# Preparing blocks 1 to 3 of the first attention earlier, loading expert weights in larger steps, and splitting a bias later

## The chip, the cores and the metric

The kernel runs on one core of a Trainium2 chip. A core has five engines that run side by side and wait for each other by semaphores: TensorE (PE in the profile; its weight loads are PEld), VectorE (DVE), ScalarE (ACT), GpSimd (POOL) and SyncE (SP), which here only starts transfers. Each engine works through its own list of instructions in order. The metric is the device time of one execution in microseconds (us). The kernel before took 1230.82 us, the median of six runs (1230.57 to 1233.02).

## The reference

The input x has four sequences of 512 tokens with 256 features. Four layers follow each other, each reading a layernorm of x and added to x:

```python
x = L0_attn_x                                    # (4, 512, 256)
x = x + L0_attn(layernorm(x), w_project, w_out)  # 16 heads of 16, causal, 512 keys
x = x + L0_ffn(layernorm(x), router_w, router_b, expert_w, expert_b)
x = x + L1_attn(layernorm(x), w_qkv, w_proj)     # over the leading axis, heads of 128
x = x + L1_ffn(layernorm(x), gate, up, down)     # weights packed in four bits
```

The second layer is a mixture of eight experts with a router for every feature: 2048 logits a token, softmax over the eight experts of each feature, the two greatest kept and made to sum to one, and the eight expert outputs added with these weights:

```python
logits = (h @ router_w.T + router_b).reshape(T, O, E)
w, sel = top_k(softmax(logits, -1), 2);  w = w / w.sum(-1, keepdims=True)
c = zeros((T, E)).at[t, sel].add(w)              # summed over the features
out = einsum("te,teo->to", c, einsum("th,eoh->teo", h, expert_w) + expert_b)
```

## The kernel before

The 2048 tokens stand in SBUF as 16 tiles of 128 rows (`xres`); four tiles make a block of 512 rows, and block j holds tokens 128j to 128j+127 of all four sequences. The first attention goes over the blocks in 44 steps, called batches in the code: 4 for block 0, 8 for block 1 and 16 each for blocks 2 and 3. All products are in float32.

Before its first step a block is prepared (`prepare`): its rows are normalised (`norm_pieces`: statistics on DVE, an inverse root by Newton steps, `rsqrt_steps`, on DVE for blocks 0 and 1 and on POOL for blocks 2 and 3, then the normalised rows `xn`), transposed on PE and evacuated as `xT0`, projected (`project`: queries and keys, two halves of two products, evacuated by ACT to `stage` and laid out in `qk` by eight transfers a half, L558) and given values (`values`, L570). The zeros and ones that stand between the heads in `qk` and `va` come from POOL (`blank`, five parts a block).

A step n then does, on PE, `greatest(n+1)` (scores whose maxima DVE takes, L633 and L653), `shift(n)` (the maxima transposed, L664, and subtracted from the queries by DVE, L669), `mask(n+1)` (the causal mask added by products, L648), some filling work, `mixed(n-1)` (probabilities times values, L719), `powers(n)` (scores again, transposed, L683), and filling work again. ACT makes the exponentials (L692) and POOL sets their masked part to zero (L702). The score tiles come from five PSUM buffers; a `greatest` and a `powers` take four each. After the last batch of a sequence `divided` transposes, divides and transposes again (L737 to L755, one buffer `oq`), and after the last sequence multiplies by `w_out` (L764) and adds to `xres`.

The order on PE, DVE and POOL is written out by hand. Filling work is a list of streams of pieces. A piece names an engine and a cost; `fill(PE=..., DVE=...)` advances a slot counter and issues pieces, earlier streams first, until the budget is spent. A piece can also ask for a number of slots since the one before it and for a condition. The streams of this stage are the preparation of the next block (put first), `fold_pieces` (the biases are added to the expert and router weights: a product of a selector with the split bias `bp`, L269, and two additions on DVE, L275, for each of eight pieces), `hidden_pieces` (the layernorm and transposes for the mixture), `logit_pieces` (L251, evacuated by ACT), `weight_pieces` (17 pieces a tile on DVE: the two greatest, and the sums), `result_pieces` (expert products, L251) and `addition_pieces`. A logit piece waits for all folds of its pair, for the weights of the tile two before, and for a count of weight pieces made. All these evacuate through `ps_dn`, two PSUM buffers that also serve the transposes and projections.

The split of the biases, three bfloat16 parts in `rows`, is made on POOL at the start (`blanks`, L521 to L532) from a 96-row array that the host lays out with the rows repeated three times. The weights of router and experts are loaded in 16 transfers of 256 KB, two after each of the first eight steps (`load_pair`), the last two blocks of x after steps 2 and 6. The order on SP is not written out: a scheduler places its transfers, and each waits for the transfer that used its semaphore before.

After the last step the second attention (L890 to L1025) runs with what is left of the mixture as filling work, a share for each of its steps that is computed from the products left, and then the last layer.

## Time and profile before

| | us |
|---|---|
| median of six runs | 1230.82 |
| the profiled execution | 1231.05 |
| its span, first to last instruction | 1229.3 |
| PE busy | 1172.2 (95%) |
| DVE busy | 812.8 (66%) |
| ACT busy | 483.7 (39%) |
| POOL busy | 131.3 (11%) |
| first scores (`greatest(0)`) start | 25.9 |
| powers of step 0, 3, 7 and 10 end | 38.2, 74.8, 114.4, 142.4 |
| first product of router logits starts | 134.7 |
| powers of step 43 end | 401 |
| weights of the second attention are loaded | from 419.9 |

The profile page gives the busy time of the engines, a strip of 40 slices, the chain of work that ended last, and the costliest groups of instructions. The trace behind it can be asked for a timeline of a stretch, for waits, and for busy times by stretches. In all of them a product of float32 counts as several PE instructions, and a PE that is shown busy may run at a lower granted clock.

### The profile page before, as it was taken

What the parts mean: (1) busy time and instruction counts of PE and PEld (TensorE: products, weight loads), DVE (VectorE), ACT (ScalarE), POOL (GpSimd) and SP (SyncE); (2) the same over time, 40 slices, a digit from 0 to 9 for tenths busy, and PEclk for the clock granted to TensorE, in tenths of its full rate; (3) what the DMA queues carried; (4) which work ended last, traced back from release to release, by engine and by line L of the source; (5) the groups of instructions that cost most, each with busy time, mean ns of one, the idle gap of its engine ahead of it and who ended that gap; (6) DMA issues with size and microseconds to landing.
All of it is one profiled execution on the core that took longest, in us unless ns stands there. A gap on an engine that the chain in (4) does not pass through costs nothing.

```text
span 1229.3 us, 18921 instructions
## 1 busy us (share of the span) xinstructions
PE 1172.2 (95%) x7278; PEld 682.4 (56%) x7278; DVE 812.8 (66%) x1862; ACT 483.7 (39%) x1101; POOL 131.3 (11%) x249
## 2 busy tenths in 40 slices
PE   6888999999999897999999999999999999999998
PEld 4656555555545443555555555555645456475487
DVE  3655589888889838395967396588589962734710
ACT  1243455555545533344444344345234431312300
POOL 7343422111121001000000000100000000000000
PEclk9899999999999988999999999999999999999999
DMA  6031102000000310000000001011010000000000
GB/s 201 6 100 35 19 1 36 1 1 2 1 2 2 116 56 1 1 1 1 1 1 1 1 1 35 10 43 53 1 50 19 1 1 17 1 1 18 0 1 35
DMA packets 19386, 26.78 MB, mean 22 GB/s; under 512 B 4992, under 2 KB 13440, under 8 KB 19040
## 3 DMA queue, kind: packets, MB, share of 16 engines
q1 hardware_dynamic: 18624, 24.40, 7.1%
q10 hardware_dynamic: 672, 1.18, 0.3%
q8 instruction: 57, 0.93, 0.3%
q14 instruction: 33, 0.27, 0.1%
HBM read 19.27 MB, written 2.10 MB: 17 GB/s over the span
## 4 chain that ended last, share of the span: by engine, by line
PE 76%; DVE 17%; ACT 3%; issue 1%; POOL 1%; DMA 0%; ACTq 0%; DVEq 0%; POOLq 0%
PE qk_ps L937 10%; PE y L1178 9%; PE g L874 9%; PE u L874 9%; PE o L1025 8%; PE lg_ps L251 7%; PE eo L251 6%; DVE mx L653 4%; PE s L633 4%; PE s L683 2%; PE v_ps L919 2%; PE qk_ps L548 2%; PE av L719 2%; PE s L950 1%; DVE lg L411 1%
## 5 line engine op out<-in xcount | busy, mean ns | idle before, releaser
L937 PE MATMUL qk_ps<-xT,wqkv 128*128 128x512 f32 x320 | 151.3, 605 | 5.1 <-ACT qT L941 5.1
L251 PE MATMUL lg_ps<-rw,xT 128*128 128x512 f32 x256 | 127.2, 620 | 4.4 <-ACT part L339 1.4
L251 PE MATMUL eo<-ew,xT 128*128 128x512 f32 x256 | 121.2, 598 | 1.9 <-ACT part L339 1.9
L1025 PE MATMUL o<-wpj,oT 128*128 128x256 f32 x512 | 119.4, 382 | 0.0
L653 DVE TENSOR_REDUCE mx<-s 128x1 f32<-128x384 f32 (+3 forms) x176 | 100.5, 633 | 18.1 <-PE s L648 18.1
L1178 PE MATMUL y<-wd,it 128*128 128x256 f32 x512 | 112.1, 379 | 0.0
L1025 PEld LDWEIGHTS o<-wpj,oT 128*128 128x128 f32 x512 | 96.0, 190 | 28.2 <-issue 16.4
L1178 PEld LDWEIGHTS y<-wd,it 128*128 128x128 f32 x512 | 97.0, 190 | 15.6 <-issue 2.9
L937 PEld LDWEIGHTS qk_ps<-xT,wqkv 128*128 128x128 f32 x320 | 59.6, 191 | 75.4 <-issue 61.8
L692 ACT ACTIVATE pt<-s 128x512 f32<-128x512 f32 (+1 forms) x176 | 83.7, 561 | 35.5 <-PE s L683 35.5
L874 PE MATMUL g<-xT,wgu 128*128 128x512 f32 x192 | 90.5, 594 | 0.0
L874 PE MATMUL u<-xT,wgu 128*128 128x512 f32 x192 | 90.2, 592 | 0.0
L702 POOL TENSOR_SCALAR_AFFINE_SELECT pt<-pt 128x256 f32<-128x256 f32 (+2 forms) x88 | 56.7, 651 | 267.2 <-ACT pt L692 266.8
L339 ACT ACTIVATE part<-eo,c 128x256 f32<-128x256 f32 x128 | 53.7, 472 | 77.3 <-PE eo L251 77.3
L1156 ACT ACTIVATE th<-sq 128x512 f32<-128x512 f32 x64 | 40.3, 630 | 88.7 <-DVE sq L1155 88.7
L251 PEld LDWEIGHTS lg_ps<-rw,xT 128*128 128x128 f32 x256 | 47.0, 196 | 50.2 <-issue 39.0
L251 PEld LDWEIGHTS eo<-ew,xT 128*128 128x128 f32 x256 | 47.1, 191 | 47.8 <-issue 40.0
L633 PE MATMUL s<-qk 32*128 32x128 f32 (+3 forms) x512 | 67.5, 500 | 2.0 <-ACT pt L692 1.9
L239 DVE TENSOR_TENSOR xres<-xres,y 128x256 f32<-128x256 f32 x16 | 6.7, 421 | 91.3 <-PE y L1178 91.3
L313 ACT COPY lg<-lg_ps 128x512 f32<-128x512 f32 x64 | 37.7, 589 | 72.5 <-PE lg_ps L251 72.5
L366 DVE TENSOR_TENSOR part<-part 128x512 f32<-128x512 f32 x32 | 21.9, 684 | 64.2 <-ACT part L339 64.1
L941 ACT COPY qT<-qk_ps 128x512 f32<-128x512 f32 x64 | 37.8, 593 | 61.5 <-PE qk_ps L937 61.5
(254 smaller groups left out, 1821.7 us busy)
## 6 DMA issues: line engine op xcount, KB each, us to landing
qk<-stage SPq DMA_DIRECT2D x56, 64.0 KB, 2.4
wqkv<-in_w_qkv SPq DMA_DIRECT2D x2, 1536.0 KB, 8.2
rw<-in_router_w SPq DMA_DIRECT2D x8, 256.0 KB, 4.4
ew<-in_expert_w SPq DMA_DIRECT2D x8, 256.0 KB, 5.2
wpj<-in_w_proj SPq DMA_DIRECT2D x1, 2048.0 KB, 15.3
out<-xres SPq DMA_DIRECT2D x4, 512.0 KB, 2.6
xres<-in_x SPq DMA_DIRECT2D x3, 512.0 KB, 7.1
dq_wgu<-in_gate_w SPq DMA_DIRECT2D x8, 128.0 KB, 2.4
```

The costliest lines, as they stand in the source:

```text
L251: nc.tensor.matmul(ps, lhsT=xT[:, hc, (g % 4) * P : (g % 4 + 1) * P], rhs=w[:, hc, 2 * pair : 2 * pair + 2, :].rearrange("p e o -> p (e o) ...
L339: nc.scalar.mul(part[:, e % 4], ps[:, i], c[:, e : e + 1])
L633: nc.tensor.matmul(tiles[h][:, b * nk : (b + 1) * nk].rearrange("p (c k) -> p c k", k=P), lhsT=queries(j, g)[r, s], rhs=qk[r, g, : j + 1, ...
L653: nc.vector.tensor_reduce(maxes[n % 2][:, :nb, h, 0], ps[:, : nb * nk].rearrange("p (b k) -> p b k", b=nb), AX.X, ALU.max,)
L692: nc.scalar.activation(pt[:, i, : nb * nk], tiles[2 * pair + i][:, : nb * nk], AF.Exp, scale=0.25)
L702: nc.gpsimd.affine_select(out=last, in_=last, compare_op=ALU.is_ge, fill=0.0, base=0, pattern=pattern, channel_multiplier=-1,)
L874: nc.tensor.matmul(ps, lhsT=wgu[:, w, half, jj, par * P : (par + 1) * P], rhs=xT[:, half, :], start=half == 0, stop=half == 1,)
L937: nc.tensor.matmul(ps, lhsT=wqkv[:, hc, kv, h, :], rhs=xT[:, hc, :], start=hc == 0, stop=hc == 1,)
L941: nc.scalar.copy(kT if h == HPK else qT[:, h, :], ps)
L1025: nc.tensor.matmul(ys[t // 2][:, t % 2], lhsT=state["o"][:, h, t * P : (t + 1) * P], rhs=wpj[:, HPK * kv + h, :], start=kv == 0 and h == 0 ...
L1156: nc.scalar.activation(th, sq, AF.Tanh, scale=0.7978845608028654)
L1178: nc.tensor.matmul(ps, lhsT=it[:, c // 2, c % 2, t * P : (t + 1) * P], rhs=wd[:, c // 2, c % 2, :], start=c == 0, stop=c == 2 * NJ - 1,)
```

## The change

- Block 1 is normalised right after block 0, on DVE, before the first step; its transposes stand between `greatest(0)` and `mask(0)`, and DVE evacuates them. Its projections and values are a stream of their own that begins between `mask(0)` and `greatest(1)`. Its `xT0` takes an unused buffer of the logits.
- The preparation of block 2 is put in at step 1 and that of block 3 at step 8, where block 2 came at step 4 and block 3 at step 12. Both use POOL for the Newton steps; values come before queries and keys; conditions hold the projections back until enough steps and blanks are done.
- `blank` has six parts a block instead of five; POOL makes two after step 0 and then one a step. `blanks` waits for the rows of block 1 rather than those of block 0.
- The bias array has 8 rows; it is loaded three times into a buffer that DVE sets to zero first. Its split, in three parts, is made on POOL after steps 1, 2 and 3, and uses buffers of the mixture.
- The weights of router and experts are loaded four transfers after each of steps 0 to 3. A fold waits for four slots after its load instead of three, and for slot 11.
- Block 2 of x is loaded at the start, before the first step.
- `hidden_pieces(0)` is put first among the streams and does its Newton steps on DVE; the two output products of block 0 lose a gap between their pieces.

```diff
@@ fold_pieces
-                    "DVE", 1.4, cond=lambda i=i, c=c: slot >= loaded.get((i, c), slot) + 3
+                    "DVE", 1.4,
+                    cond=lambda i=i, c=c: slot >= max(loaded.get((i, c), slot) + 4, 11),
@@ hidden_pieces
-        yield from norm_pieces(b, b1, b2, out, cond=lambda: b < 2 or done in halves)
+        yield from norm_pieces(
+            b, b1, b2, out, eng=None if b else nc.vector, cond=lambda: b < 2 or done in halves
+        )
@@ blank
-            if i == 4:
+            if i == 5:
                 to = va.shape[1] if j == NBLK - 1 else (j + 1) * per_block
                 nc.gpsimd.memset(va[:, j * per_block : to], 1.0)
-                nc.gpsimd.memset(keys[96:97], 1.0)
@@ the bias buffer
-        bs = a3.tile([P, 2, 512], F32, tag="pt", name="bs")
-        nc.sync.dma_start(out=bs[0:96], in_=bias)
+        bs = b1.tile([P, 2, 512], F32, tag="hi4", name="bs")
+        nc.vector.memset(bs, 0.0)
@@ blanks, and the new bias_pieces
-            for i in range(5):
+            for i in range(6):
                 blank(1, i)
+        def bias_pieces():
             d = bs[0:96, 0]
...
             nc.gpsimd.tensor_copy(bp[0:32], bh[0:32])
+            yield
             nc.gpsimd.tensor_tensor(br, d, bh, ALU.subtract)
...
             nc.gpsimd.tensor_copy(bp[64:96], br[64:96])
+            yield
             for i in range(8):
                 nc.gpsimd.tensor_copy(sel[:, i, :], mask32[:, i : i + 1].to_broadcast([P, P]))
@@ prepare, cut into three
+        def inputs_T(j, xn, xT):
             for hc in range(2):
                 yield need("PE", 0.5, 1 - hc)
-                ps = transposed(out[0], hc, ps_dn, "dn", f"x0_ps{j}_{hc}")
-                nc.scalar.copy(
+                ps = transposed(xn, hc, ps_dn, "dn", f"x0_ps{j}_{hc}")
+                copy = nc.vector.tensor_copy if j == 1 else nc.scalar.copy
+                copy(
...
+        def projections(j, xT):
+            if j > 1:
+                for s in (0, 2):
+                    yield need("PE", 1.75, s == 0, cond=lambda: blanked > 6 * j - 12)
+                    values(j, xT, s)
             for half in range(2):
...
                 for i in range(2):
-                    yield need("PE", 1.75, 0 if half or i else 1)
+                    yield need(
+                        "PE", 1.75, 0 if half or i else 1,
+                        cond=lambda: j < 2 or done >= 8 * j - 12 and blanked >= 6 * j - 6,
+                    )
                     project(j, xT, half, stage, i)
-                if half == (not j):
+                if half == (not j) and j < 2:
...
+        def prepare(j):
+            out = []
+            yield from norm_pieces(
+                j, b1, b2, out, cond=lambda: j == 2 or inputs[2].next is None
+            )
+            xT = a1.tile([P, 2, NS, P], F32, tag="xT0", name=f"xT0_{j}")
+            yield from inputs_T(j, out[0], xT)
+            yield from projections(j, xT)
@@ divided
-                yield need("PE", 1.75, 1)
+                yield need("PE", 1.75, 1 if j or not t else 0)
...
-                yield need("DVE", 0.7, 1)
+                if j:
+                    yield need("DVE", 0.7, 1)
...
-            streams.insert(fold_at, Stream(hidden_pieces(j)))
+            streams.insert(fold_at if j else 0, Stream(hidden_pieces(j)))
@@ before the first step
-        for piece in prepare(0):
+        both = [[], []]
+        for j in range(2):
+            for piece in norm_pieces(j, b1, b2, both[j], eng=nc.vector):
+                pass
+            normed.clear()
+            if not j:
+                xT = a1.tile([P, 2, NS, P], F32, tag="xT0", name="xT0_0")
+                for piece in inputs_T(0, both[0][0], xT):
+                    pass
+        blanks(both[1][0])
+        for piece in projections(0, xT):
             pass
         greatest(0)
+        xT = unused("xT0_1", "p (h s q) -> p h s q", h=2, s=NS)
+        for piece in inputs_T(1, both[1][0], xT):
+            pass
         mask(0)
+        inputs = {1: Stream(projections(1, xT))}
...
+        for i in range(3):
+            nc.sync.dma_start(out=bs[32 * i : 32 * i + 8], in_=bias)
+        load_x(2)
+        split = bias_pieces()
+        fill(PE=2.0, DVE=0.0)
@@ the steps
-            if (not n or batches[n - 1][0] != j) and j + 1 < NBLK:
-                inputs = Stream(prepare(j + 1))
-                streams.insert(0, inputs)
+            if n in (1, 8):
+                to = 2 if n == 1 else 3
+                inputs[to] = Stream(prepare(to))
+                streams.insert(0, inputs[to])
...
-            if n < 8:
-                w, dram = (rw, router_w) if n < 4 else (ew, expert_w)
-                load_pair(w, dram, 2 * n % 8)
-                load_pair(w, dram, 2 * n % 8 + 1)
-                loaded[n // 4, n % 4] = slot
-            if 1 <= n < 11:
-                blank(2 + (n - 1) // 5, (n - 1) % 5)
-            if n in (2, 6):
-                load_x(n // 4 + 2)
+            if n < 4:
+                w, dram = (rw, router_w) if n < 2 else (ew, expert_w)
+                for i in range(4):
+                    load_pair(w, dram, 4 * n % 8 + i)
+                    loaded[n // 2, (4 * n % 8 + i) // 2] = slot
+            for _ in range(1 + (not n) if n < 11 else 0):
+                blank(2 + blanked // 6, (blanked + 5) % 6)
+                blanked += 1
+            if n:
+                next(split, None)
+            if n == 6:
+                load_x(3)
```

## The prediction

> **What bounds the kernel now.** I read the page's busy times first, then busy times by stretches, cut at the ends of steps (step n ends with its powers, the PE group at L683), then the timeline of the poor stretches. The page says that PE is the engine to save:
>
> ```profile
> PE 1172.2 (95%) x7278; PEld 682.4 (56%) x7278; DVE 812.8 (66%) x1862; ACT 483.7 (39%) x1101; POOL 131.3 (11%) x249
> ```
>
> The busy times by stretches (PE, PEld, DVE, ACT, POOL, granted clock, DMA share, GB/s) show where it isn't full:
>
> ```profile
> 0.00:25.90 25.90, 16.71 (x46) 8.76 (x46) 9.45 (x33) 4.89 (x8) 19.04 (x23) 1.00 0.74 231
> 25.90:74.00 48.10, 42.98 (x497) 32.24 (x500) 25.19 (x57) 13.96 (x27) 19.25 (x25) 0.89 0.17 34
> 74.00:114.30 40.30, 33.63 (x434) 23.76 (x430) 23.33 (x53) 12.85 (x26) 16.05 (x23) 0.92 0.24 59
> 142.30:216.50 74.20, 72.95 (x765) 42.74 (x761) 61.68 (x157) 39.94 (x104) 20.01 (x42) 1.00 0.09 16
> 216.50:401.00 184.50, 175.87 (x1862) 95.07 (x1859) 157.98 (x375) 99.61 (x269) 29.03 (x56) 0.99 0.01 2
> 401.00:500.00 99.00, 85.29 (x333) 41.42 (x326) 61.60 (x177) 41.76 (x111) 8.93 (x32) 0.91 0.15 54
> 500.00:1229.30 729.30, 718.93 (x3046) 421.52 (x3045) 458.53 (x980) 258.21 (x534) 7.91 (x30) 1.00 0.04 12
> ```
>
> From 500 us on PE has no gap worth naming, so a time won before it is won at the end, unless it is spent between. From 142 to 401 PE and DVE are both near full (DVE 220 of 259 us). In steps 0 to 7 (25.9 to 114.4) PE idles or runs at half clock. Two stretches of granted clock, and one stall in the timeline:
>
> ```profile
> 29.70:36.50 6.80, 6.80 (x61) 5.94 (x60) 4.19 (x8) 0.00 (x0) 5.73 (x13) 0.50 0.01 2
> 39.90:43.20 3.30, 3.30 (x36) 3.01 (x37) 2.96 (x11) 0.30 (x1) 1.55 (x2) 0.50 0.03 5
> ```
>
> ```profile
> 81.19 0.66 PE L737 MATMUL av_T<-ident,avs 128*128 128x128 f32 x4
> 84.07 0.55 PE L752 MATMUL oq_T<-ident,oq 128*128 128x128 f32 x2 [2.22 <-DVE oq L744]
> ```
>
> DVE was at block 2's statistics and PE had nothing else to do: the folds and logits that could fill wait for late weights.
>
> **A measure.** PE's work at full clock, from the timeline and the chain: a pair of 128x512 products 1.72 us, values 1.73, four transposes 0.59, a greatest 1.10, sixteen mask products 0.88, mixed 1.01, powers 1.10. In program order, PE from the first greatest to the powers of step 7 holds 59.6 us of such work, and takes 114.4 - 25.9 = 88.5 us: 28.9 are lost. In the changed program's order the same stretch holds 66.9: the same steps and, besides, block 2's values (3.46), its second half of projections (3.44) and two folds. So two sums decide: what is lost in this stretch, and what later stretches do with the 7.3 us of work done ahead.
>
> **The start, to 25.9 us: 0.** The added memset on DVE (128x1024; the 128x1088 one took 0.96) delays block 0's rows from 11.4 to about 12.3, but their transposes start at 12.95, behind PE's warm-up products. Its price is 0 to 0.96; I take 0, as the slack is 1.5. Block 1's statistics and Newton steps (about 6.5 us, like block 0's 4.87 to 11.4) run on DVE to 18.5, where DVE was idle until 29.5. POOL's blanks now start at 18.5 instead of 11.5 and end at 31.4; the first transfers of `qk` wait only for an older memset, block 1's wait for the second blank (23) and are not issued before 36. The smaller bias transfers and the missing early weight loads free DMA that nothing here waits for: 0.
>
> **Steps 0 and 1.** After `greatest(0)` (25.9 to 29.1, held by its transfers as before) PE has block 1's transposes (1.2), mask, two projections (3.44), `greatest(1)`, `shift`, mask, values (3.46) and powers. I charge one window of half clock, 3.4 us (row two above), so 1.7 lost; powers of step 0 end at 43.9 (before: 38.2). Two more projections, `greatest(2)`, shift, mask, mixed, powers: step 1 ends at 52.1 (before: 48.0).
>
> TensorE's granted clock fell at 29.7 although the largest idle gap before it was 0.9 us. [...]
>
> **Step 2: a new wait.** Block 2's Newton steps are now on POOL in front of the masking of step 1's exponentials. DVE gets to block 2's statistics after the maxima of step 2, at 52.5, and ends them at 55.2 (4 x 0.53 + 0.6). POOL's ten steps take 2.8 (83.54 to 86.3 in the timeline), so the masking (2.15) runs 58.1 to 60.2, where the exponentials were ready at 53.7. PE waits in `mixed(1)` from 55.8 to 59.3. Step 2 ends at 62.1 (before: 62.3), with 4.7 lost.
>
> **Steps 3 to 7.** One of the two `ps_dn` buffers is held by transposed values that DVE has not yet divided, so transposes, projections, values and folds pass through one buffer and wait for ACT's copy each time (0.59): 2.4 lost in step 3, which ends at 74.2 (before: 74.8). Step 4 has no filling work and runs at the pace of its chain, 6.1 (before: 79.41 to 81.26 after the same wait for maxima); end 80.3 (81.3). In steps 5 and 6 folds come in pairs through that buffer: the second waits for the first's two additions (1.28), or for ACT behind four exponentials (2.06). I count 4.0 and 1.9 lost; ends 93.4 (90.7) and 103.5 (104.6). Step 7: 1.95 lost, end 113.5 (114.4). POOL's split (6.3 us with its blank ahead of step 2's masking, 5.9 ahead of step 3's) ends 3.5 and 0.7 us before PE needs the result: 0.
>
> Lost from 25.9 to here: 2.1 + 1.9 + 0.4 + 4.7 + 2.4 + 1.4 + 4.0 + 1.9 + 1.95 = 20.75, against 28.9. The gain is 0.9 in time and 7.3 in work. Three steps on, with like losses, step 10 ends at 139.9 (before: 142.4) with five pairs of logits instead of two and block 3's transposes done, 6.4 of work: 8.9 us. The bounds of the lost sum: 13 if the steps ran like those of 142 to 216 (about 1 us lost a step, eight steps, and the 5 of steps 0 and 2), 29 if waits grow to what they were.
>
> **Expert loads: 0.** In the changed order SP issues 16 loads (0.5 each, landing in 4.4 to 5.2 by the DMA rows) behind block 1's 16 small transfers, from about 51 to 62; they have landed by 70, the first fold comes at 82, and the next transfer on SP is due at 88. The cover for this is 12 us.
>
> **Steps 11 to 43: passed on.** The first tile's logits begin at 119 instead of 134.7. But block 3's preparation then takes PE's filling work in steps 11 to 14, and the second tile's logits end in step 17 instead of 13. DVE's order counts it: weight instructions done ahead of step 14, 17, 20 and 43 are 31, 37, 59 and 220; before 12, 31, 53 and 211. So DVE starves in steps 14 to 18 and is still six ahead at 20, nine at 43 (some 0.85 us each). In between both engines carry nearly what they carried: PE 147 us from step 20 to 43 instead of 151, DVE three weight instructions more. I take 8.9 as passed on. Bounds: 4 if DVE alone set the pace (only the 3.9 in time at step 20 would count), 13 if DVE's nine instructions also shorten its waits in 401 to 500 us, where PE lost 13.7.
>
> **The sum.** 1231.05 - 8.9 = 1222.2 for the profiled execution; it lies 0.2 above the median of the six runs, so 1222.
>
> **The rivals.** *Gain spent* : DVE sets the pace from 143 to 434. For: the chain of waits there is largely DVE's (11.8% of the first 300 us in L653 alone); DVE 86% busy. Against: PE was as full. If only the 2.5 us in time count and DVE's starving costs 2: 1230.
>
> *Slower, by POOL's queue*: masking stands behind Newton steps, blanks and split in steps 1 to 3. POOL's instructions stretch beside DVE: L174 took 1.10 instead of 0.20 in one place, and DVE's own copy L92 took 3.41 beside POOL. If the Newton steps take 4.6 (as they did at 478.5) and the split twice its time (5 us more in each of two steps, beyond slacks of 3.5 and 0.7), PE loses 1.8 + 1.5 + 4.3, and two windows of half clock, 3.4, with it: 11. That ends at 1233, and with the DVE-paced stretch at 1237. It decides from 9 us of stretch on. Against: in the trace the split ran at 0.6 to 1.5 an instruction.
>
> *More*: the eight steps lose 13 or DVE's lead is worth its waits after 401: 1212 to 1215.
>
> *The weights are late*: they would have to land 12 us later than I count; then the folds stall as before and the time is 1229.
>
> **How the numbers follow.** Gain passed on 0.55 (1216 to 1229), more 0.10, gain spent 0.16, weights late 0.03, slower 0.16. About 0.2%, 2.5 us (1228.4 to 1233.3), is what a measurement tells from no change. Faster: 0.53 of the first, 0.10, and a third of the spent cases, 0.68; same: the ends of the first 0.02, the other spent cases 0.11 and late weights 0.03, 0.16; slower: 0.16. The range takes in all but the ends of the first and last: 1211 to 1234.
>
> **What would show it.** Right: PE's clock near 1 from 37 us on; `mixed(1)` starting at 59 behind POOL's masking; step 7 ending at 113 to 114 and the first logits starting at 117 to 121; step 10 ending near 140; SP idle before block 2's transfers. Wrong: step 7 ending after 118; DVE's idle time in steps 14 to 18 over 15 us; `mixed(2)` or `mixed(3)` waiting for POOL; PE's busy share after 500 us below what it was. The prediction fails above all if step 43 ends later than 401.

## The result and the profile after

The changed kernel takes 1235.55 us, the median of 34 runs, against 1232.92 us, the median of 69 runs of the kernel before. The ratio is 1.0025 with a 95% interval of 1.0019 to 1.0032: the change made the kernel slower by a quarter of a percent, 2.6 us between the medians. The prediction had 1222, faster.

The profiled execution of the changed kernel took 1237.64 us, 2.1 above its median; its span is 1235.9 us. That of the kernel before took 1231.05, 1.9 below the median of its 69 runs, so the two spans differ by 6.6 us where the medians differ by 2.6. The busy line of its page, as in the kernel before: PE is still the engine to save, and is even fuller, 1181.6 us instead of 1172.2 for the same 7278 instructions.

```profile
PE 1181.6 (96%) x7278; PEld 684.4 (55%) x7278; DVE 818.9 (66%) x1875; ACT 481.8 (39%) x1099; POOL 129.2 (10%) x239
```

The busy times by stretches of the changed kernel, cut at the start, at the ends of steps 3, 7, 10, 20 and 43, and where PE becomes full (us, then PE, PEld, DVE, ACT and POOL busy, the granted clock, DMA share, GB/s):

```profile
0.00:25.60 25.60, 16.78 (x50) 8.83 (x50) 15.74 (x59) 4.92 (x8) 12.07 (x18) 1.00 0.53 161
25.60:77.00 51.40, 46.17 (x532) 34.56 (x532) 23.41 (x45) 14.74 (x28) 29.05 (x34) 0.90 0.41 107
77.00:121.50 44.50, 37.36 (x420) 23.82 (x420) 26.20 (x54) 13.19 (x28) 14.23 (x20) 0.92 0.10 16
121.50:155.80 34.30, 29.39 (x316) 17.32 (x314) 21.22 (x51) 12.93 (x26) 11.29 (x19) 0.90 0.07 13
155.80:239.90 84.10, 78.24 (x754) 44.24 (x755) 57.41 (x150) 40.16 (x108) 17.55 (x31) 0.96 0.08 14
239.90:426.40 186.50, 179.47 (x1852) 97.43 (x1852) 157.51 (x376) 99.99 (x271) 28.64 (x56) 0.98 0.01 2
426.40:520.00 93.60, 86.88 (x356) 43.49 (x353) 64.95 (x179) 42.16 (x108) 8.53 (x32) 0.98 0.16 57
520.00:1235.90 715.90, 707.34 (x3015) 414.71 (x3013) 452.41 (x965) 253.70 (x525) 7.81 (x30) 1.00 0.04 12
```

The kernel before in its steps 8 to 10, same columns:

```profile
114.40:142.40 28.00, 25.86 (x321) 16.81 (x322) 14.92 (x36) 12.45 (x25) 11.13 (x19) 1.00 0.17 39
```

The reader is to see two things. The stretch of steps 8 to 10 (121.5 to 155.8), and the one of steps 11 to 20 behind it, now have idle PE and a granted clock of 0.90 and 0.96, where the kernel before had a clock of 1.00 in both and an almost full PE in steps 11 to 20. And the stretch behind step 43, where the kernel before had PE busy for 85.3 of 99 us at 0.91, is now at 86.9 of 93.6 and 0.98. The loss lies in front of step 43 and a large part of it comes back behind it. The ends of the steps say how much (us; a step ends with its powers):

| step | before | predicted | changed kernel |
|---|---|---|---|
| 0, 1, 2 | 38.3, 48.0, 62.3 | 43.9, 52.1, 62.1 | 43.0, 52.0, 62.2 |
| 3 | 74.8 | 74.2 | 77.0 |
| 5 | 90.7 | 93.4 | 100.7 |
| 7 | 114.4 | 113.5 | 121.5 |
| 8 | 122.5 | | 136.3 |
| 10 | 142.4 | 139.9 | 155.8 |
| 13 | 164.2 | | 184.0 |
| 20 | 216.7 | | 239.9 |
| 43 | 401.1 | by 401 | 426.4 |
| end of the span | 1229.3 | | 1235.9 |

Steps 0 to 2 end within a microsecond of the forecast. From there the changed kernel falls 25.3 us behind the kernel before, and wins back 18.7 behind step 43.

**Where PE loses it.** The timeline of step 5 (start, duration, engine, line, instruction, and in brackets the idle time before it and what ended it) shows the two folds that follow each other through one buffer:

```profile
83.58 0.66 PE L760 MATMUL av_T<-ident,avs 128*128 128x128 f32 x4
84.07 0.38 PE L775 MATMUL oq_T<-ident,oq 128*128 128x128 f32 x2
...
85.92 0.38 PE L270 MATMUL fold<-rows 128*128 128x512 bf16 x1 [1.47 <-ACT aT L778]
...
86.33 1.28 DVE L276 TENSOR_TENSOR rw<-rw,fold 128x512 f32<-128x512 f32 x2 [2.67 <-PE fold L270]
87.77 0.59 PE L270 MATMUL fold<-rows 128*128 128x512 bf16 x1 [1.47 <-DVE rw L276]
```

The first fold waits 1.47 us for ACT's copy of `oq_T`, the second 1.47 us for DVE's additions of the first, because the other buffer holds `av_T` until DVE divides it. So much was in the prediction. What it left out of step 5 is the clock behind such gaps. Busy times of the changed kernel in slices of 3 us (same columns):

```profile
60.00:63.00 3.00, 3.00 (x41) 2.63 (x37) 2.59 (x4) 1.27 (x3) 2.91 (x3) 0.51 0.96 311
...
66.00:69.00 3.00, 2.97 (x23) 2.04 (x24) 0.00 (x0) 0.59 (x1) 2.94 (x3) 0.65 0.67 255
...
88.00:91.00 3.00, 3.00 (x22) 1.86 (x21) 1.28 (x2) 0.00 (x0) 0.17 (x1) 0.50 0.00 0
91.00:94.00 3.00, 3.00 (x11) 1.76 (x10) 2.97 (x6) 0.00 (x0) 0.00 (x0) 0.50 0.00 0
127.00:130.00 3.00, 1.55 (x6) 0.97 (x7) 2.97 (x7) 1.27 (x2) 0.00 (x0) 0.72 0.00 0
130.00:133.00 3.00, 3.00 (x4) 0.76 (x3) 2.76 (x12) 0.00 (x0) 0.00 (x0) 0.50 0.00 0
133.00:136.00 3.00, 3.00 (x61) 2.22 (x64) 0.01 (x1) 0.96 (x2) 0.00 (x0) 0.64 0.00 0
```

Step 8 was not priced by itself. Its timeline in the changed kernel: DVE normalises the rows of the first mixture block ahead of the subtraction and the maxima of the step, and one of the four instructions takes 1.97 us, beside a memset of POOL, where two others take 0.40 and 0.41. PE stands in front of the transposes, then in front of their copies, then in front of the logits, which run at half clock (3.78 us for a pair that takes 1.98 at full clock):

```profile
123.74 3.18 DVE L211 TENSOR_SCALAR xn<-xres,ln_mv,ln_rs 128x256 f32<-128x256 f32 x4
...
124.18 1.94 POOL L484 MEMSET qk<- 1x2048 f32 x1
...
124.82 0.28 PE L227 MATMUL xT_ps<-ident,xn 128*128 128x128 f32 x1
...
126.33 0.97 PE L227 MATMUL xT_ps<-ident,xn 128*128 128x128 f32 x3 [1.24 <-DVE xn L211]
...
127.98 0.83 PE L227 MATMUL xT_ps<-ident,xn 128*128 128x128 f32 x4 [0.68 <-ACT xT L297]
...
129.58 3.78 PE L251 MATMUL lg_ps<-rw,xT 128*128 128x512 f32 x4 [0.78 <-ACT xT L295]
```

And in step 13 the held buffer is seen by itself. `av_T` is written at 171.8, DVE divides it at 178.2, behind weight work and four maxima, and the second projection of block 3, which has the operands, waits for that buffer:

```profile
171.76 0.66 PE L760 MATMUL av_T<-ident,avs 128*128 128x128 f32 x4
...
176.05 1.94 DVE L676 TENSOR_REDUCE mx<-s 128x1 f32<-128x384 f32 x4
...
178.19 0.42 DVE L767 TENSOR_TENSOR oq<-av_T,rden 128x256 f32<-128x256 f32 x1
...
178.76 3.00 PE L554 MATMUL qk_ps<-xT,wp 128*128 128x512 f32 x4 [2.73 <-DVE oq L767]
```

**Waits that are shown as busy time.** PE is busy 9.4 us longer in the changed kernel, with the same 7278 instructions. Half clock gives little of it: without its last stretch at the end, each of the two traces has 40.9 us at 0.50, with PE busy for 39.8 us of them in the changed kernel and 38.7 in the kernel before, so by estimate half a microsecond more. More comes from this: the four products of a `greatest` work on 32 rows of PE each (32*128 in the rows below) and overlap when their four score buffers are free. In block 3 its eight instructions of 0.64 us then take 1.14 us together. When ACT's exponentials still hold the buffers (those from 303.35 to 305.39 beside the first row below), the products follow each other, and the `greatest` takes 2.4 to 3.7 us from the first start to the last end, nearly all of it recorded as busy (seven of the 16 in the changed kernel; in the kernel before four, of 2.1 to 2.8). Two timeline rows of the changed kernel:

```profile
303.65 2.43 PE L656 MATMUL s<-qk 32*128 32x512 f32 x8
...
320.50 1.14 PE L656 MATMUL s<-qk 32*128 32x512 f32 x8
```

The groups by form (instructions, busy us, mean ns) give it for all 16 such steps, first before:

```profile
L633 PE MATMUL s<-qk 32*128 32x512 f32 x128 | 23.9, 640 | 0.0
```

and then of the changed kernel:

```profile
L656 PE MATMUL s<-qk 32*128 32x512 f32 x128 | 30.2, 641 | 0.6 <-ACT pt L715 0.6
```

The mean of one instruction is the same, the union of their times is not: 16 x 1.14 = 18.2 us would be free of waits, so 5.7 us were hidden in it before, and 12.0 are now (a little of it is half clock: one of the 16 runs partly at 0.50). The column of idle time shows 0.0 and 0.6 of them.

### The profile page after: what moved, and what is told of

It reads as the page before. It is cut to its first block, busy times and chain, and to the rows that moved or that the text cites. A ratio compares the mean times of both kernels' runs of the same rounds, so it can differ in the third digit from the quotient of the medians.

```text
span 1235.9 us, 18938 instructions
## 1 busy us (share of the span) xinstructions
PE 1181.6 (96%) x7278; PEld 684.4 (55%) x7278; DVE 818.9 (66%) x1875; ACT 481.8 (39%) x1099; POOL 129.2 (10%) x239
## 4 chain that ended last, share of the span: by engine, by line
PE 75%; DVE 12%; ACT 3%; issue 1%; POOL 0%; ACTq 0%; DVEq 0%; POOLq 0%
PE qk_ps L986 10%; PE y L1227 9%; PE g L923 9%; PE u L923 9%; PE o L1074 8%; PE lg_ps L251 7%; PE eo L251 7%; DVE mx L676 3%; PE s L656 3%; PE s L706 2%; PE av L742 2%; PE s L999 1%; PE v_ps L968 1%; PE o L787 1%; PE a L1057 1%
## 5 line engine op out<-in xcount | busy, mean ns | idle before, releaser
L251 PE MATMUL eo<-ew,xT 128*128 128x512 f32 x256 | 123.8, 607 | 4.0 <-ACT part L342 1.6
L725 POOL TENSOR_SCALAR_AFFINE_SELECT pt<-pt 128x256 f32<-128x256 f32 (+2 forms) x88 | 53.2, 609 | 284.3 <-ACT pt L715 284.0
L692 DVE TENSOR_TENSOR qk<-qk,mxT 128x128 f32<-128x128 f32 (+2 forms) x44 | 15.2, 345 | 92.5 <-PE mxT L687 92.3
L251 PEld LDWEIGHTS eo<-ew,xT 128*128 128x128 f32 x256 | 46.7, 192 | 50.8 <-issue 38.3
L656 PE MATMUL s<-qk 32*128 32x128 f32 (+3 forms) x512 | 72.8, 482 | 1.3 <-ACT pt L715 1.2
L923 PEld LDWEIGHTS u<-xT,wgu 128*128 128x128 f32 x192 | 36.5, 190 | 45.9 <-issue 44.7
## 6 DMA issues: line engine op xcount, KB each, us to landing
wpj<-in_w_proj SPq DMA_DIRECT2D x1, 2048.0 KB, 15.4
```

Source lines behind the costliest of these rows:

```text
L251: nc.tensor.matmul(ps, lhsT=xT[:, hc, (g % 4) * P : (g % 4 + 1) * P], rhs=w[:, hc, 2 * pair : 2 * pair + 2, :].rearrange("p e o -> p (e o) ...
L656: nc.tensor.matmul(tiles[h][:, b * nk : (b + 1) * nk].rearrange("p (c k) -> p c k", k=P), lhsT=queries(j, g)[r, s], rhs=qk[r, g, : j + 1, ...
L725: nc.gpsimd.affine_select(out=last, in_=last, compare_op=ALU.is_ge, fill=0.0, base=0, pattern=pattern, channel_multiplier=-1,)
L923: nc.tensor.matmul(ps, lhsT=wgu[:, w, half, jj, par * P : (par + 1) * P], rhs=xT[:, half, :], start=half == 0, stop=half == 1,)
```

## The experiments

For the comparison I use three numbers of each run's profile: the ends of steps, PE's work done by the end of step 43 (program order from the end of `greatest(0)`, with the full-clock durations of the prediction's measure), and from these what PE loses, relative to the kernel before: up to step 43 (end of step 43 less work done) and after it (rest of the span plus work done, since the whole work is the same). For the changed kernel: 426.4 - 309.7 = 116.7 against 401.1 - 308.0 = 93.1, 23.6 more lost up to step 43; 809.5 + 309.7 = 1119.2 against 828.2 + 308.0 = 1136.2, 17.0 less lost after it; together the 6.6 us by which the spans differ. A profile is a single execution. Up to step 7, e13 has the same order of work as the kernel before, and ends it at 111.3 instead of 114.4; so a difference of up to three microseconds between two profiles is not read. The profiles of e1, e6 and e12 lie 4.6, 2.7 and 3.0 us above the medians of these runs. Runs e13 to e16 stand further below.

| run | median us | ratio to before, 95% | steps 3, 7, 13, 20, 43 end | work by 43 | lost to 43 | lost after |
|---|---|---|---|---|---|---|
| before | 1232.92 | | 74.8, 114.4, 164.2, 216.7, 401.1 | 308.0 | 0 | 0 |
| changed | 1235.55 | 1.0025, 1.0019 to 1.0032 | 77.0, 121.5, 184.0, 239.9, 426.4 | 309.7 | +23.6 | -17.0 |
| e1 layernorm back | 1242.85 | 1.0093, 1.0070 to 1.0115 | 76.5, 120.9, 177.4, 228.8, 411.8 | 304.6 | +14.1 | +2.3 |
| e2 block 3 back | 1242.01 | 1.0083, 1.0063 to 1.0103 | 74.2, 118.7, 175.7, 234.1, 416.2 | 302.9 | +20.2 | -11.5 |
| e3 folds apart | 1231.53 | 0.9993, 0.9974 to 1.0011 | 74.3, 112.8, 178.1, 233.9, 420.5 | 309.7 | +17.7 | -17.1 |
| e4 Newton on DVE | 1238.88 | 1.0056, 1.0039 to 1.0073 | 78.0, 122.5, 185.0, 240.9, 427.4 | 309.7 | +24.6 | -17.1 |
| e5 products in the gap | 1232.56 | 0.9996, 0.9981 to 1.0012 | 76.8, 121.3, 183.2, 236.9, 422.0 | 309.7 | +19.2 | -17.0 |
| e6 loads back | 1231.12 | 0.9985, 0.9971 to 0.9998 | 76.5, 117.3, 180.1, 236.0, 421.0 | 309.7 | +18.2 | -15.4 |
| e7 divide at once | 1218.92 | 0.9887, 0.9866 to 0.9908 | 71.3, 107.0, 161.8, 215.1, 400.8 | 313.2 | -5.5 | -7.2 |
| e8 e7 and folds apart | 1228.53 | 0.9966, 0.9949 to 0.9984 | 72.2, 111.0, 168.8, 222.8, 408.7 | 313.2 | +2.4 | -5.5 |
| e9 before, divide at once | 1220.56 | 0.9906, 0.9888 to 0.9923 | 71.4, 107.7, 158.7, 213.7, 395.4 | 309.7 | -7.4 | -2.3 |
| e10 e7, products later | 1223.01 | 0.9922, 0.9907 to 0.9937 | 72.2, 107.8, 161.0, 215.9, 401.7 | 313.2 | -4.6 | -3.4 |
| e11 block 2 back | 1223.19 | 0.9921, 0.9906 to 0.9936 | 64.1, 106.4, 163.3, 213.1, 395.8 | 302.9 | -0.2 | -7.6 |
| e12 e11 and divide at once | 1225.34 | 0.9920, 0.9890 to 0.9950 | 65.3, 103.1, 154.6, 218.2, 401.7 | 309.7 | -1.1 | -1.5 |
| e17 block 2's products later | 1235.16 | 1.0016, 1.0003 to 1.0028 | 73.9, 116.5, 179.5, 232.8, 412.8 | 299.4 | +20.3 | -15.3 |
| e18 e11 and folds apart | 1223.75 | 0.9920, 0.9903 to 0.9937 | 63.6, 103.8, 163.0, 212.8, 394.0 | 302.9 | -2.0 | -5.3 |

The theory that I began with (A): PE loses its time in steps 3 to 10, where more work now passes through two buffers, one of them held, and behind DVE. The rival (B): DVE's mixture work is starved in steps 11 to 20. Each edit below is against the changed kernel where nothing else is said.

**e1 and e2: two of the moves undone.**

```diff
-            b, b1, b2, out, eng=None if b else nc.vector, cond=lambda: b < 2 or done in halves
+            b, b1, b2, out, cond=lambda: b < 2 or done in halves
...
-            streams.insert(fold_at if j else 0, Stream(hidden_pieces(j)))
+            streams.insert(fold_at, Stream(hidden_pieces(j)))
```

> The changed kernel with one part undone: the layernorm of the first mixture block stands behind the other filling work again and makes its Newton steps on POOL (the first router logits then stand in step 9 instead of step 8). Theory A (the stretch of steps 3 to 10 is long because DVE work and PSUM buffers stand in front of PE there; PE stands still 1.5 us for the normalised rows in step 8 and then runs at half clock): step 8 shrinks from 14.8 us to 9 to 10, step 43 ends at 420 to 422, total 1229 to 1232. Theory B (what is lost is lost by DVE's mixture work starting late and being starved in steps 11 to 20): the logits start later, so nothing is gained, step 43 ends at 426 to 430 and the total is 1235 to 1238.

```diff
-            if n in (1, 8):
+            if n in (1, 12):
```

> The changed kernel with block 3's preparation put in at step 12 again instead of step 8, so that the second tile's logits stand in steps 10 to 12 and the preparation in steps 14 to 17. Theory B (DVE starved in steps 11 to 20 while PE does the preparation, and PE then waits in turn): the ten microseconds of steps 11 to 20 come back, step 20 ends at 228 to 232 instead of 239.9, total 1225 to 1229. Theory A (the loss is in steps 3 to 10 and these steps only carry it): step 20 ends at 236 to 240, total 1233 to 1237.

Both misses are instructive. Without the early layernorm step 8 shrinks to 6.5 us (120.9 to 127.4) and step 43 ends 14.6 us earlier, more than the 4 to 6 that theory A had, and yet the kernel is 7.3 us slower (1242.85 against 1235.55): by then it has done 5.1 us less work, and after step 43 it loses 19.3 us more. With block 3 back at step 12, steps 11 to 20 take hardly less (82.5 us from step 10 to 20 against 84.1), and the total is 6.5 us worse; theory B's ten microseconds don't come back (step 20 ends at 234.1, between the two forecasts). So the early layernorm and the early block 3 are both gains within the changed kernel, and the end of step 43 alone is no measure of it.

**e3 and e6: the folds.** Set one slot apart, or spread by loading two transfers a step again (with the folds from slot 10 on):

```diff
-                    "DVE", 1.4,
+                    "DVE", 1.4, 1,
```

> The changed kernel with the folds asking for one slot between them, so that a slot holds one fold instead of two or three. Steps 5 to 7 then hold 2, 2 and 1 folds instead of 4, 3 and 1. If the folds that follow each other through one buffer cost steps 5 and 6 what they exceeded my chain by (7.2 and 0.5 us): step 6 ends at 104 to 107 instead of 111.3, total 1228 to 1232. If the waits in step 5 come from elsewhere (transposes, projections and folds would be held by the same buffer however the folds lie): step 6 ends at 109 to 112, the later folds cost steps 8 and 9 as much, total 1234 to 1237.

```diff
-            if n < 4:
-                w, dram = (rw, router_w) if n < 2 else (ew, expert_w)
-                for i in range(4):
-                    load_pair(w, dram, 4 * n % 8 + i)
-                    loaded[n // 2, (4 * n % 8 + i) // 2] = slot
+            if n < 8:
+                w, dram = (rw, router_w) if n < 4 else (ew, expert_w)
+                load_pair(w, dram, 2 * n % 8)
+                load_pair(w, dram, 2 * n % 8 + 1)
+                loaded[n // 4, n % 4] = slot
...
-                    cond=lambda i=i, c=c: slot >= max(loaded.get((i, c), slot) + 4, 11),
+                    cond=lambda i=i, c=c: slot >= max(loaded.get((i, c), slot) + 4, 10),
```

> The changed kernel with the expert weights loaded two transfers after each of the first eight steps again; the folds then lie 2, 1, 1, 1, 1, 1, 1 in steps 4 to 10 instead of 4, 3, 1 in steps 5 to 7. If the four-step loads harm only through the folds that they let come in a bunch: step 7 ends at 111 to 114 instead of 121.5, and as with the folds set apart the total is 1229 to 1232. If the loads two by two on SP also delay the transfers of the projections or the folds come too late for the logits: step 10 ends at 152 or later and the total is 1233 or more.

1231.53 and 1231.12: either edit takes away 4.0 to 4.4 us. In e3 step 7 ends at 112.8, 8.7 us earlier (1.6 of them already at step 0), and 2.8 of that are given back in steps 8 to 10, which now hold folds. The four-step loads harm through the bunch of folds that they let come, as expected; in e6 step 7 ended later than expected (117.3, not 111 to 114).

**e4: block 2's Newton steps on DVE.**

```diff
-                j, b1, b2, out, cond=lambda: j == 2 or inputs[2].next is None
+                j, b1, b2, out, eng=nc.vector if j == 2 else None,
+                cond=lambda: j == 2 or inputs[2].next is None
```

> The changed kernel with block 2's Newton steps on DVE instead of POOL, so that the masking of step 1's exponentials no longer stands behind them. If that wait (3.5 us on PE in step 2, with the half clock behind it) is a cause of the late steps 2 and 3: step 3 ends at 72 to 74 instead of 77.0 and the total is 1231 to 1233. If step 2 is held by DVE all the same (ten more instructions of DVE, about 1.5 us, between the maxima of step 2 and the shift of step 3): step 3 ends at 76 to 78 and the total stays at 1234 to 1237.

1238.88, 3.3 us worse, and worse than both expectations. Steps 2 and 3 take 27.3 us instead of 25.0. Moving the Newton steps to DVE does not take the delay of steps 2 and 3 away; there they stand in front of the shift and the maxima themselves.

**e5: the half clock in step 8.** Two spare products fill PE's gap in front of the transposes.

```diff
+        for i in range(ahead):
+            nc.tensor.matmul(
+                ps.rearrange("p t q -> p (t q)"), lhsT=ident, rhs=spare_rhs[0],
+                start=True, stop=True,
+            )
...
-            ps = transposed(out[0], hc, ps_dn, "dn", f"xT_ps{b}_{hc}")
+            ps = transposed(out[0], hc, ps_dn, "dn", f"xT_ps{b}_{hc}", 2 if not b and not hc else 0)
```

> The changed kernel with two spare products of 128x512 on PE (1.7 us at full clock; their result is overwritten) ahead of the first transposes of the mixture, where PE stands still from 124.8 to 126.33 for the normalised rows and then runs at half clock to about 135. If the idle gap itself brings the half clock and the half clock is what makes step 8 long: PE's granted clock stays near 1 from 126 to 135, step 8 takes 11 to 12 us instead of 14.8, total 1231 to 1233. If step 8 is held by DVE and ACT however fast PE runs: it takes 14.5 to 15.5 us, total 1235 to 1237.

1232.56, 3.0 us won by adding 1.7 us of work. The timeline and the slices of e5, to be held against those of the changed kernel above:

```profile
124.63 1.94 PE L227 MATMUL xT_ps<-wp,ident 128*128 128x512 f32 x4
...
126.40 0.71 PE L232 MATMUL xT_ps<-ident,xn 128*128 128x128 f32 x4
...
127.79 0.66 PE L232 MATMUL xT_ps<-ident,xn 128*128 128x128 f32 x4 [0.68 <-ACT xT L302]
...
130.13 1.98 PE L256 MATMUL lg_ps<-rw,xT 128*128 128x512 f32 x4 [1.69 <-DVE oq L773]
```

```profile
127.00:130.00 3.00, 0.77 (x5) 0.42 (x4) 2.97 (x8) 1.27 (x2) 0.00 (x0) 1.00 0.00 0
130.00:133.00 3.00, 2.87 (x36) 1.49 (x36) 2.59 (x12) 0.59 (x1) 0.00 (x0) 1.00 0.00 0
133.00:136.00 3.00, 2.04 (x45) 1.62 (x38) 0.00 (x0) 2.06 (x5) 0.54 (x1) 1.00 0.02 5
```

The transposes start when they did (126.40, 126.33), but the clock stays at 1.00, the logits take 1.98 instead of 3.78, and step 8 takes 12.9 us instead of 14.8 (11 to 12 were expected). The half clock there is lost time, and with the gap filled it did not come.

**e7: the held buffer.** DVE divides in the slot of the transposes, ahead of the next subtraction and maxima instead of behind them.

```diff
-            yield need("DVE", 0.7, 1)
+            yield need("DVE", 0.7)
             nc.vector.reciprocal(rden, ps[:, :, 16])
```

> The changed kernel with DVE's division of the transposed values in the same slot as the transposes instead of the next one, so that the one of the two buffers that they hold is free some 4 us earlier for folds, projections, transposes and logits. Theory A (PE loses its time where this work passes through one buffer): lost time in steps 3 to 13 falls by 6 to 12 us, step 13 ends at 172 to 178 instead of 184, total 1225 to 1230. Rival (PE and DVE wait for each other at the division instead, or the buffer is not what these steps wait for): step 13 ends at 181 to 186, total 1234 to 1238.

1218.92: 16.6 us below the changed kernel, and 1.1% below the kernel before (ratio 0.9887), the fastest kernel here of those that leave nothing out. Step 13 ends 22 us earlier. The projection of step 13 that waited 2.73 us, in e7:

```profile
153.18 0.66 PE L760 MATMUL av_T<-ident,avs 128*128 128x128 f32 x4
...
154.47 0.42 DVE L767 TENSOR_TENSOR oq<-av_T,rden 128x256 f32<-128x256 f32 x1
...
158.13 1.98 PE L554 MATMUL qk_ps<-xT,wp 128*128 128x512 f32 x4 [0.46 <-ACT aT L778]
```

The buffer is held for 1.7 us instead of 6.9 (from the start of the transposes to the end of the division). The busy times of e7 for its start to step 3, steps 4 to 7 and 8 to 10: clock 0.96, 1.00 and 0.94 instead of 0.90, 0.92 and 0.90.

```profile
25.60:71.30 45.70, 42.62 (x534) 32.20 (x534) 23.85 (x45) 15.13 (x29) 27.72 (x33) 0.96 0.45 121
71.30:107.00 35.70, 33.42 (x419) 22.22 (x417) 28.14 (x64) 13.38 (x28) 15.65 (x22) 1.00 0.10 17
107.00:137.90 30.90, 28.59 (x319) 16.67 (x319) 20.75 (x42) 13.08 (x26) 11.15 (x19) 0.94 0.11 19
```

The edit also lets the second transposes come half a step earlier, so products change places behind it (folds 4, 2, 2 in steps 5, 6 and 8). The 16.6 us are of the edit as a whole.

**e8 and e12: do the losses add up?** e8 is e7 with the folds one to a slot from slot 10; e12 is e7 with block 2 back at step 4 (the edit of e11).

```diff
-                    "DVE", 1.4,
-                    cond=lambda i=i, c=c: slot >= max(loaded.get((i, c), slot) + 4, 11),
+                    "DVE", 1.4, 1,
+                    cond=lambda i=i, c=c: slot >= max(loaded.get((i, c), slot) + 4, 10),
...
-            yield need("DVE", 0.7, 1)
+            yield need("DVE", 0.7)
```

> The division at once, and the folds one to a slot from slot 10 on (steps 4 to 9). If the bunched folds and the held buffer are separate losses they add up (4 us measured for the folds, 6 to 12 expected for the buffer): total 1221 to 1227, faster than the kernel before. If they are the same loss: no better than the better of the two alone, 1228 to 1232.

> Block 2's preparation at step 4 again and the division at once. Alone they bring 12.4 us (1223.19) and 16.6 us (1218.92) from the changed kernel. If both take away the same loss (block 2's transposes, values, projections and the folds pass in steps 3 to 6 through the buffer that the division holds), the two together bring hardly more than the better one: 1216 to 1221. If they are two losses (the early preparation delays steps 2 and 3 behind POOL and DVE, the buffer delays steps 5 to 13), they add up: 1206 to 1212.

1228.53 and 1225.34 (1217.69 to 1228.38): neither adds up. In e8 other products move into steps 7 to 10 with the folds, and it lies 9.6 above e7. The profile of e12, of the slowest of its six runs, is fast up to step 13 (154.6, the earliest of all) and then takes 63.6 us for steps 14 to 20, where e7 takes 53.3 for 5.1 us less work. No run of e12 comes near the 1206 to 1212 of two separate losses: the held buffer and block 2's early preparation are not that.

**e9: the same edit on the kernel before.**

> The kernel before with the same edit as e7: DVE's division in the slot of the transposes. In the kernel before, steps 3 to 7 lose 12.2 us of PE and steps 8 to 13 only 3, with half as much work through the two buffers there. Theory A (the changed kernel packs more work through the buffer that is held, so the buffer costs it more): the kernel before gains 3 to 8 us from the edit, 1225 to 1230, and the change, with the buffer free, is worth the difference to 1218.9, 6 to 11 us, near the 8.9 predicted. Rival (the held buffer cost both kernels the same): 1214 to 1219, and the change is worth nothing even with the buffer free.

1220.56, between the two expectations and nearer the rival's: the kernel before gains 11 to 12 us (its median is 1231.73 in the runs beside e9, 1232.92 in all). The buffer cost both kernels, the changed one 4 to 5 us more. With it free the change is worth 1220.56 - 1218.92 = 1.6 us, from four runs of each, whose ranges touch (1220.17 to 1221.31, 1218.34 to 1220.50).

**e10: half clock behind step 43.** e7 with three spare products ahead of the first transposes of the second attention's first two blocks.

```diff
-            yield from into_T(out, xT, f"xT1_{j}")
+            yield from into_T(out, xT, f"xT1_{j}", 3 if j < 2 else 0)
```

> The kernel of e7 (division at once) with three spare products of 128x512 on PE ahead of the first transposes of the first and the second block of the second attention, where PE stands still for the normalised rows 2.9 and 2.65 us and then runs at half clock (0.80 and 0.85 in 420 to 440, 0.83 in 460 to 470). If the half clock there is lost time of its own: total 1215 to 1217. If DVE and ACT set the pace of that stretch all the same: 1218 to 1220.

1223.01, 4.1 us slower than e7 and above both expectations. But the edit did not fill both gaps. The first three products fill the first (0.24 us of idle PE are left where e7 has 2.91); the logits behind it still wait for ACT's copy, now 1.28 us instead of 0.72, and the clock falls all the same, at 430.78. The gap of 2.65 us stands in front of other transposes and stayed; the second three products came 18 us later, where PE waited for nothing:

```profile
427.26 1.73 PE L232 MATMUL xT_ps<-ident,xn 128*128 128x128 f32 x8 [0.24 <-DVE xn L211]
...
463.56 1.80 PE L232 MATMUL xT_ps<-ident,xn 128*128 128x128 f32 x8 [2.65 <-DVE xn L211]
```

```profile
482.00 2.74 PE L227 MATMUL xT_ps<-rw,ident 128*128 128x512 f32 x6
```

So 2.6 of the 4.1 us are plain added work (three products of 0.86), and whether the half clock there is lost time of its own stays open.

**e11, e17, e18: block 2.**

```diff
-            if n in (1, 8):
-                to = 2 if n == 1 else 3
+            if n in (4, 8):
+                to = 2 if n == 4 else 3
```

> The changed kernel with block 2's preparation put in at step 4 again instead of step 1. Steps 3 to 5 lose its transposes, values and projections, which go to steps 6 to 9 and push logits to step 10 and block 3 to steps 11 to 15. If preparing block 2 early is what makes steps 2 to 5 late (POOL's Newton steps ahead of the masking, then the one buffer): step 5 ends at 90 to 94 and the total is 1229 to 1233. If early work is good in itself and only passes badly through the buffer, undoing it moves the loss to steps 6 to 15, as undoing block 3 and the layernorm did: 1238 to 1244.

1223.19, 12.4 us better than the changed kernel, 9.7 better than the kernel before, and better than either theory had it. Steps 1 to 3 take 23.0 us instead of 34.0, for 4.6 us less work. The stretch from the start to step 3 in e11, at full clock:

```profile
25.60:64.10 38.50, 37.41 (x507) 27.80 (x503) 17.18 (x30) 12.20 (x24) 23.03 (x20) 1.00 0.49 127
```

With the division at once it is the other way round: there the early block 2 gains 6.4 us (e12 1225.34, e7 1218.92). What the early preparation of block 2 is worth thus hangs on how long the buffer is held.

Next, e17 leaves the normalisation and transposes early and holds only the products back; e18 sets e11's folds apart.

```diff
-                    yield need("PE", 1.75, s == 0, cond=lambda: blanked > 6 * j - 12)
+                    yield need(
+                        "PE", 1.75, s == 0,
+                        cond=lambda: blanked > 6 * j - 12 and (j > 2 or done >= 6),
+                    )
```

> The changed kernel with block 2 normalised and transposed as early as there, but its values held back until six steps are done; its products then lie in steps 6 to 9 (values 6, projections 7 to 9), nearly where e11 has them (7 to 9). e11 moved normalisation and products back and gained 12.4 us. If the products in steps 3 to 7 are the harm (they pass between folds and divisions through one buffer): 1222 to 1228. If the early normalisation is the harm (DVE's statistics and POOL's Newton steps in steps 2 and 3, transposes in step 3): 1232 to 1237.

> e11 (block 2's preparation at step 4) with the folds one to a slot, 2 each in steps 5, 6, 8 and 9. e11 lost 14.2 us in steps 3 to 7, and the folds set apart gave the changed kernel 4.0. If the bunched folds cost e11 the same: 1217 to 1221. If what they cost was bound up with block 2's products beside them: 1222 to 1226.

e17: 1235.16, no gain. Steps 1 to 3 lose 11.7 us as in the changed kernel (10.6), where e11 loses 4.2. So in steps 1 to 3 it is the normalisation, with its transposes, that harms, not the products; with the reserve that holding the products back also pushes the logits a step later, which e1 showed to cost. That is 6.4 us. By the same measure PE loses 14 us less in steps 8 to 20 in e11 than in the changed kernel, and e17 does not say why. e18: 1223.75, nothing won over e11: the bunched folds are no loss of their own without block 2 beside them.

**e13 to e16: does DVE's pace spend the lead?** Six of the seven running sums a tile are left out, in four kernels.

```diff
-                if e < NE - 1:
+                if e < 1:
                     less = b5.tile([P, HID], F32, tag="owing", name=f"owing_{g}_{e}")
```

> The kernel before with six of the seven running sums a tile left out (96 of DVE's instructions, 0.42 us each and 0.68 from one to the next, 65 us in all; the mixture weights are then not the reference's), nothing else moved. This and the next three are read as pairs. If DVE's pace in steps 11 to 43 spends the work that the change does ahead (theory C), DVE made lighter by a fifth lets it through: the changed kernel, 2.7 us slower than the kernel before, becomes 2 to 8 us faster in this pair. If its loss is all PE's own waits in steps 2 to 13 (theory A), the changed kernel stays 1 to 5 us slower. The kernel before itself: 1215 to 1231.

> The changed kernel with the same instructions left out. Theory C: 2 to 8 us below e13. Theory A: 1 to 5 us above e13.

> The kernel of e9 (before, division at once) with the same instructions left out. Between e9 and e7 the change was worth 1.6 us. Theory C: here it is worth 5 to 9 us, near the work that e7 has done more by step 13 (8.1 us of PE, 3.1 us later). Theory A: 0 to 3 us, as with the whole of DVE's work.

> The kernel of e7 (the change, division at once) with the same instructions left out. Theory C: 5 to 9 us below e15. Theory A: 0 to 3 us below e15.

| pair | before | changed | changed less before | the same with all of DVE's work |
|---|---|---|---|---|
| as they are | 1225.52 | 1223.48 | -2.0 | +2.6 |
| division at once | 1213.97 | 1206.96 | -7.0 | -1.6 |

Both pairs fall into the ranges of theory C: a lighter DVE makes the change worth 4.7 and 5.4 us more. The single executions spread by 2 to 6 us, so the shift in one pair is not sharp; that both go the same way by the same amount is the evidence. In the spans of the second pair it is only 2.8 (1219.6 to 1216.6, against 1211.2 to 1205.4). And in steps 14 to 20 e16 loses as much as e7 (11.5 and 10.4 us; e15 and e9 5.6 and 7.5), so that DVE's pace is not what spends the lead there; that is left open. The lighter DVE pays in steps 21 to 43: they take 10.0 and 7.1 us less in the changed kernels (186.6 to 176.6, 185.7 to 178.6), and 0.4 and 2.3 less in the kernels before, each time with the same work of PE.

## Why the prediction was wrong

**The start and steps 0 to 2: right.** Ends at 43.0, 52.0 and 62.2 (43.9, 52.1, 62.1). POOL's Newton steps ran from 54.2 to 57.0 and the masking behind them, and `mixed(1)` started in two parts at 58.1 and 59.1, where I had 59.3. What was not drawn from it is that these 4.7 us and the 2.4 of step 3 are the price of preparing block 2 early, and that they could exceed what is had for it: e11 and e17 put 6.4 us of harm there.

**Lost from 25.9 to step 7, 20.75: wrong, it is 29.0** (121.5 - 25.6 = 95.9, less the 66.9 of work). It is the upper bound that I gave ("29 if waits grow to what they were"), as much as the kernel before loses. Most is in two terms: step 3, 14.8 instead of 12.1 us, and step 5, 17.0 instead of 13.1. The waits in them were named (one `ps_dn` buffer, folds in pairs); what they set off was not: half clock from 60 to 63, partly from 66 to 72, and from 88 to 94. At half clock the transposes of `av` in step 2 take 1.11 us (0.66 at 76.91), eight mask products 1.06 (0.61 at 80.02) and a pair of projections 3.21 (1.98 at 95.52). I had charged half clock once, to steps 0 and 1.

**"Three steps on with like losses": wrong.** Steps 8 to 10 took 34.3 us where I had 26.4. The early layernorm on DVE had no term in the sum. In step 8 it stands in front of the shift and the maxima, PE waits for it (1.24 us), and the clock falls to 0.50 at 128.33; e5 prices the clock alone at 3.0 us. But to take the layernorm back costs 7.3 us (e1): the term was missing, and yet is worth its price.

**Steps 11 to 43, "8.9 passed on": wrong.** At step 10 there was no gain left to pass on: the changed kernel is 13.4 us later and has 6.4 of work ahead, 7.0 lost instead of 8.9 won. At step 43 it has lost 23.6, so these steps cost another 16.6 that I had put at nothing. The held buffer goes on there (step 13's 2.73 us), and `greatest` waits for score buffers. Even with the division at once the lead goes: at step 13 e7 is 3.1 us later than e9 with 8.1 of work ahead, at step 43 5.4 later with 3.5. DVE's pace spends part of it, in steps 21 to 43 (e13 to e16); the rival "gain spent" was right in so far.

**After step 43: the gain was undersized.** I took the nine instructions of DVE's lead as worth nothing in the sum, and in the bound of 13 as worth 4. The kernel loses 17.0 us less there. With it the account closes: 15.9 us beyond the forecast up to step 10 (7.0 lost instead of 8.9 won) and 16.6 in steps 11 to 43, less these 17.0, are but for rounding the 15.4 us between the forecast of 1222.2 and the profiled 1237.64. The gain does not hang on what was lost before: the changed kernel, e3, e4 and e5 have one order of PE's work from step 10 on and lose 17.0 to 17.1 less. Which part of the order does it is open: e7 is further ahead in DVE's work when step 43 ends (225 instructions of the weights, 217 in the changed kernel, 209 in the kernel before) and gains only 7.2.

**Expert loads 0 and the split 0: right**, but for the folds: the loads set when the folds come, and that they come in a bunch costs the changed kernel 4.0 to 4.4 us (e3, e6). **The rival "slower, by POOL's queue"** reached the measured time, 1233 to 1237, for another reason: the Newton steps and the masking on POOL kept their durations (2.8 and 2.14 us), and moving the Newton steps off POOL made it worse (e4). **The test** that I put first, the end of step 43, was a poor one: e1 comes nearer to it than the changed kernel (411.8 against 426.4) and is slower.

In sum: three steps of the prediction failed. The waits behind the held buffer were charged too little, with the half clock behind them (0.50 from 88 to 94; 29.0 us lost instead of 20.75 up to step 7); steps 8 to 10 were taken over "with like losses" and took 34.3 us instead of 26.4; and the gain was taken as passed on where another 16.6 went. As the kernels are, the change costs 2.6 us; with the division at once it is worth 1.6, with the lighter DVE 2.0, with both 7.0. So, to a microsecond or two, the buffer takes 4 to 5 of it and DVE's pace about 5, whichever of them goes first. That 7.0 lies near the 8.9 predicted is no confirmation: it is another order of work, with 96 instructions of DVE left out. The bunched folds are not a loss beside that (e8, e18), and the half clock came with the waits (a clock of 0.92 in steps 4 to 7 of the changed kernel, 1.00 in those of e7).

## What to carry to other kernels

Work moved ahead of need is worth what the buffers on its way let through: count who holds each of them and until when, before counting the work. Here one division standing behind four maxima cost the two kernels 11 to 12 and 17 us, more than the 1.6 that the change is worth without it, or the 7 with a lighter DVE. And when order is written by hand, judge an edit at the end of the span, with the work done by each mark beside the time: a stretch that ends 14 us earlier had done less and lost more behind it.

## What was not expected of the hardware

TensorE's granted clock fell after short waits. In step 8 of the changed kernel gaps of 1.24 and 0.68 us came before the clock fell to 0.50 at 128.33 (the one of 0.78 us came behind it). In e5, at the same place, gaps of 0.68 and 1.69 us left it at 1.00, so here a single gap's length does not decide. In the traces of the two kernels the half clock comes in stretches of 3.41 or 6.83 us (but for the last of each trace), with starts a whole number of 3.41 us apart; in the changed kernel they begin at 29.34, 60.06, 66.89, 87.37 and 128.33, and so on. In the 3.41 us ahead of the fall at 128.33 PE was idle for 1.91 us, in two such stretches of e5 for 0.68 and 1.69 (columns as above; first the changed kernel, then e5):

```profile
124.92:128.33 3.41, 1.50 (x9) 0.77 (x7) 3.41 (x6) 0.58 (x1) 1.21 (x1) 1.00 0.22 37
```

```profile
124.76:128.17 3.41, 2.73 (x12) 1.41 (x12) 3.41 (x6) 0.59 (x1) 1.18 (x1) 1.00 0.23 39
128.17:131.58 3.41, 1.73 (x7) 0.72 (x5) 3.27 (x11) 0.69 (x1) 0.00 (x0) 1.00 0.00 0
```

So at this place the clock fell behind the stretch with the most idle time in sum. Elsewhere that sum does not decide either. In the changed kernel the clock fell at 456.01 behind a stretch with 1.31 us of idle PE, and at 391.16 behind one with 0.27 us, in which a `greatest` with waits in its busy time runs (387.99 to 391.66). It stayed at 1.00 behind 1.95 us in e5 (from 459.26 on) and behind 1.71 us in the kernel before (from 787.41 on). In step 5 the clock fell at 87.37, in the second of the two gaps of 1.47 us at the buffers and behind 2.54 us of idle PE in 3.41; in step 8 the first wait is for DVE's normalised rows. By what rule the clock falls, and where its bound lies, these runs don't show.

The other is how a wait can hide in busy time: a `greatest` of 1.14 us takes up to 3.7 us, 3.4 of them recorded as busy, when its buffers come free one by one, and of the 30.2 us of that group nearly 12 were waiting. It also bears on the prediction's remark that the clock of the kernel before fell at 29.7 with no idle gap over 0.9 us ahead of it, from PE's first instruction at 8.05 on: `greatest(0)` stands right before as 3.17 us busy, where the measure has 1.10.

```profile
25.90 3.17 PE L633 MATMUL s<-qk 32*128 32x128 f32 x32
```
